# Two attention layers on one core: output's deep weights made in one batch in attention, pairs of exponentials summed by transfers, output's first difference in place, one pool of twelve buffers

## The chip, the cores and the metric

The kernel runs on one core of a Trainium2 chip. The metric is the time of one execution on the device in microseconds; a version's time is the median of its runs. Engines are named as in the profile: PE (TensorE, matmuls), DVE or VectorE, ACT or ScalarE, POOL or GpSimd (here it only issues transfers that add to their destination), SP (SyncE, issues all other transfers).

## The reference

Eight images of 512 channels and 32 x 32 positions, float32, go through two layers. Both do the same: group normalisation over 8 groups, query, key and value projections of 512 x 512, attention with 8 heads of 64 channels over 1024 positions, an output projection with bias, and a residual.

```python
xn = xn * norm_gamma[None, :, None, None] + norm_beta[None, :, None, None]
qkv = jnp.einsum('oc,bchw->bohw', qkv_w, xn) + qkv_b[None, :, None, None]
q, k, v = (qkv[:, 0], qkv[:, 1], qkv[:, 2])
attn = jax.nn.softmax(jnp.einsum('bhds,bhdt->bhst', q, k) * scale, axis=-1)
out = jnp.einsum('bhst,bhdt->bhds', attn, v).reshape(B, C, H, W)
return x + jnp.einsum('oc,bchw->bohw', proj_w, out) + proj_b[None, :, None, None]
```

## The kernel before

One image in one layer is a job; the 16 jobs run in the order (image 0, layer 0), (1, 0), (0, 1), (1, 1), (2, 0) and so on, numbered 0 to 15. Job n passes through three stages on PE.

*V phase* (`v_phase`). The value projection is a two-by-two Strassen-Winograd product: seven products of half matrices, in two banks of PSUM called z, y, v, u in the profile (L494).

*Deep phases* (`deep_phases`, L574 on). Output of job n-1 (called O), then K and Q of job n, each as a two-level product of that kind: seven chains, in the order OUTER = 1, 2, 6, 5, 7, 3, 4, of seven inner products each (L636, two matmuls of 128x256). A chain's result is a part, a tile p of 128x1024, put together from PSUM by ScalarE copies (L646, L648) and VectorE adds of a shared piece s5 (L653, L655). The parts are then added up: for K and Q by VectorE into quarters of k and q (`add`, L667); for O onto the residual x (`more`, L676), by VectorE (L684) or by a transfer that accumulates, issued on POOL (L682, x<-p in the profile). Each chain's left side is a weight tile w of 7 x 128 columns, 448 KB: the *deep weights*. They are fetched ahead on SP (`fetch`, w<-deep). The first time that a kind and layer are used they do not exist yet: then `prepare` makes each of them from loaded blocks by four VectorE adds of 128x128 in the deep phase itself, and stores it for later jobs (deep<-w). The right sides need sums of quarters: for K and Q `deep_steps` (L423 to L429, 128x768, made in attention), for O the class `OutputSums` (os, L534 to L539) and four half-size differences `combine` (L380 to L391) of the attention output q into a tile to.

*Attention* (`Attention`, L850 on). 64 steps: 8 groups (a pair of heads and a half of the positions) by 8 blocks kc of 128 keys. A step is: scores (L878, PE), the exponential e of 128x1024 (L883, ACT), values into the bank po (L909, PE, two steps later: LEAD = 2), and on VectorE acc += e, the softmax's sum (L893 for the first pair, L895 after). With a group's last step `finish` (L914) reduces acc (L925), copies half of po to px on ACT (L931) and adds px and the other half into q (L932: the "q add" below, after which the bank po is free). Every second group the sums are gathered on SP (r<-r), inverted (L956, L957), spread, and q is multiplied by them (L986).

Side work is placed on the 64 steps as *chores*, by `put(step, fn)` in the main loop (L1284 on): raw loads and first-level factors of weights (`first_factors`), the normalisation of the next job, `sums`, `deep_steps`. Work after an attention is ordered by a clock written by hand: `later(at, fn)` sets a due time, `advance(us)` is called after PE's work. So every engine's order is fixed in the program; an instruction that waits holds up what is behind it on its engine. Buffers: `epool` has LEAD + 4 = 6 tiles of 128x1024 for e and p, `ring` has RING = 7 tiles for w.

At the end (`last_proj`) the last job's output is made by a one-level product.

Of the kernel before, what the change touches and what calls it, by code (L numbers as in the profile page):

```python
# [46 lines left out]
RING = 7  # L47
BLOCK = {1: (0, 0), 2: (0, 1), 4: (1, 1)}

# [23 lines left out]
def fast_path(  # L73
# [13 lines left out]
    epool = ctx.enter_context(tc.tile_pool(name="epool", bufs=LEAD + 4))  # L87
# [3 lines left out]
    ring = ctx.enter_context(tc.tile_pool(name="ring", bufs=RING))  # L91
# [70 lines left out]
    def store_factors(w, layer, which):  # L162
        keep = wdram.tile([P, NW, 2, CH], F32, name=f"keep_{which}_{layer}")
        if (which, layer) == (O, 1):
            nc.sync.dma_start(keep, w)
        else:
            for s in (slice(S1, NW), slice(S3, S3 + 1)):
                nc.sync.dma_start(keep[:, s], w[:, s])
        factors[which, layer] = keep
# [3 lines left out]
    def fetch():  # L173


        if not plan or len(held) == RING:
            return
        key = plan.popleft()
        n, which, o = key
        layer = jobs[n][1]  # L180
        w = ring.tile([P, NW, P], F32, tag="w", name=f"w_{which}_{n}_{o}")
        held[key] = w
        if (which, layer, o) in deep:
            nc.sync.dma_start(w, deep[which, layer, o])
        else:
            if o in BLOCK:
                src = raw_block(layer, which, *BLOCK[o])
            else:
                src = factors[which, layer][:, FACTOR[o]]
            nc.sync.dma_start(wide(w), src)  # L190
            if which != V:
                raw.add(key)

    def prepare(key):
        if key not in raw:
            return
        raw.discard(key)
        n, which, o = key
        w = held[key]
        for part in range(4):  # L200
            factor(w, part)
        keep = wdram.tile([P, NW, P], F32, name=f"deep_{which}_{jobs[n][1]}_{o}")
        deep[which, jobs[n][1], o] = keep
        later(1.0, lambda: nc.sync.dma_start(keep, w))

# [194 lines left out]

    def inner_sums(part, direct):
# [141 lines left out]
    class OutputSums:  # L543
# [6 lines left out]
        def steps(self, c):  # L550
            def first():
                n = self.n
                if c == 2:
# [15 lines left out]
                self.pair = sums_of_four(right(self.src, to[0], OUTER[c]), slots)  # L569
# [4 lines left out]
    def deep_phases(n, extra, outs=None, early=()):  # L574
# [5 lines left out]
        chains = [(which, o) for which in ((O, K, Q) if outs else (K, Q)) for o in OUTER]  # L580
        tiles = {}

        def job(which):
            return n - 1 if which == O else n

        def begin(c):
# [3 lines left out]
            if o == OUTER[0] and which != O:  # L590
                name = "k" if which == K else "q"
                dst[which] = acts.tile([P, NC, S], F32, tag=name, name=f"{name}_{n}")
                (kt if which == K else qt)[0] = dst[which]
# [3 lines left out]
            if which == O and c in (3, 4):  # L597
                soon.extend(outs.steps(c + 2))
            e = epool.tile([P, 2, HALF], F32, tag="e", name=f"p_{n}_{c}")
            tiles[which, o] = e  # L600
            s5 = small.tile([P, QT], F32, tag="s5", name=f"s5_{n}_{c}", bufs=3)
            half = (c + len(chains)) % 2
            ends = c + 1 == len(chains)
            names = "yvzu" if ends else ("vyuz", "zyuv")[(c // 2) % 2]
            z, y, u, w = (bank(half, b, f"{b}d_{n}_{c}")[:, :QT] for b in names)
            if which == O:
                r = right(outs.src, to[0], o)
                sums = outs.at[c]
# [26 lines left out]
            def product(i, ps, start):  # L635
                nc.tensor.matmul(  # L636
# [4 lines left out]
            def put(oo, ph, ps):  # L641
                to_ = e[:, oo, ph * QT : (ph + 1) * QT]
# [16 lines left out]
        def end(c):  # L659
# [7 lines left out]
            def add(to_, a, b):  # L667
                outer.append(lambda: nc.vector.tensor_add(to_, a, b))  # L668

            if which == O:  # L670
# [3 lines left out]
                def more(oh, sh, part, moved=False):  # L674
# [5 lines left out]
                    def go():  # L680
                        if moved:
                            nc.gpsimd.dma_start(to_, p(part), accum_op=ALU.add)  # L682
                        else:
                            nc.vector.tensor_add(to_, to_, p(part))  # L684
                        parts[oh, sh] -= 1
# [7 lines left out]
                    waiting[oh, sh] += 1  # L693
                    if not moved:
# [11 lines left out]
                elif o == 6:  # L706
                    add(p(6), p(6), p(1))
# [4 lines left out]
                elif o == 7:  # L712
                    add(p(7), p(7), p(6))
# [7 lines left out]
            d = dst[which]  # L721

            def quarter(oh, sh):
                return d[:, 2 * oh : 2 * oh + 2, sh * HALF : (sh + 1) * HALF]

            if o == 2:
                add(quarter(0, 0), p(1), p(2))
            elif o == 6:
                add(p(6), p(6), p(1))
            elif o == 5:  # L730
                add(quarter(0, 1), p(6), p(5))
            elif o == 7:
                add(p(7), p(7), p(6))
                add(quarter(1, 1), p(7), p(5))
            elif o == 3:
                add(quarter(0, 1), quarter(0, 1), p(3))
            elif o == 4:
                add(quarter(1, 0), p(7), p(4))
# [5 lines left out]
        def thunk(c, j):  # L744
            def go():
                if j == 0:
# [3 lines left out]
                if order[j] in (7, 3):  # L750
# [13 lines left out]
                advance(0.43)  # L764

            return go

# [8 lines left out]
        return [thunk(c, j) for c, j in at]  # L776

    def last_weights(n):
        w = acts.tile([P, NW, 2, CH], F32, tag="deep", name="w_last")
        nc.sync.dma_start(w, factors[O, jobs[n][1]])  # L780
# [77 lines left out]
    class Attention:  # L858
        def __init__(self, n):
# [6 lines left out]
            self.es, self.acc, self.po = {}, {}, {}  # L866

# [20 lines left out]
        def add(self, i):  # L888
            g, kc = self.steps[i]
            acc, e = self.acc, self.es[i]  # L890
# [3 lines left out]
            elif kc > 1:  # L894
                nc.vector.tensor_add(acc[g], acc[g], e)  # L895

        def values(self, i):
# [6 lines left out]
            e = es.pop(i)  # L904
            for h in range(2):
# [8 lines left out]
        def finish(self, g):  # L914
# [4 lines left out]

            n, q, m = self.n, self.q, g % 2  # L920
            hp, sh = self.groups[g]
            to_ = q[:, hp, sh * HALF : (sh + 1) * HALF]
# [6 lines left out]
            p = self.po.pop(g)  # L929
            px = apool.tile([P, HALF], F32, tag="px", name=f"px_{n}_{g}")  # L930
            nc.scalar.copy(px, p[:, 0, :])  # L931
            nc.vector.tensor_add(to_, p[:, 1, :], px)  # L932
# [52 lines left out]
            def normalise():  # L985
                nc.vector.tensor_mul(place, place, box[0])  # L986

            times = (0.0, 0.2, 2.0, 4.0) if ends else (0.0, 7.6, 7.7, 16.2)
# [3 lines left out]
        def run(self, chores):  # L992
# [6 lines left out]
            if 2 in chores:  # L999
                chores[2]()  # L1000
            for i in range(3, len(steps) + LEAD):
# [3 lines left out]
                g, kc = steps[i - LEAD]  # L1005
                if kc == NT - 1:
                    self.finish(g)
                    advance(0.85)
                if i in chores:
                    chores[i]()  # L1010
                advance(1.71)

# [20 lines left out]

    def out_sums(n, outs):
# [3 lines left out]
        def start():  # L1038
            to[0] = acts.tile([P, 4, 2, HALF], F32, tag="k", name=f"to_{n}")
            combine(outs.src, to[0], 0)  # L1040

        def part(i):
            return lambda: combine(outs.src, to[0], i)

        c0, c1, c2, c3, c4 = (outs.steps(c) for c in range(5))
        steps = c0 + [start] + c3 + c1 + [part(1)] + c2 + [part(2)] + c4 + [part(3)]
        times = (0.1, 1.0, 2.5, 4.5, 5.5, 6.5, 7.5, 8.6, 14.0, 15.8, 16.5, 17.5, 19.2, 21.0)
# [20 lines left out]
    def extend_plan(n):  # L1068
        plan.extend((n, V, o) for o in ORDER)
        plan.extend((n - 1, O, o) for o in ORDER)  # L1070
# [32 lines left out]

    def first_factors(put, which_layers):

        box = []

        def start():
            box.append(acts.tile([P, 2, NW, 2, CH], F32, tag="deep", name=f"raw_{len(factors)}"))
            for i, (which, layer) in enumerate(which_layers):  # L1110
                load_blocks(box[0][:, i], layer, which)

        put(2, start)
        at = 9
        for i, (which, layer) in enumerate(which_layers):
            for part in range(4):
                at += 3
                put(at, lambda i=i, part=part: factor(box[0][:, i], part))
            put(at + 1, lambda i=i, which=which, layer=layer: store_factors(
                box[0][:, i], layer, which  # L1120
            ))
# [162 lines left out]
    for n in range(-1, len(jobs)):  # L1284
        last = n + 1 == len(jobs)
        outs = None
        if n >= 0:
            chores = {}

            def put(i, fn):  # L1290
                while i in chores:
                    i += 1
                chores[i] = fn

            if last:
                w = last_weights(n)
                for i, fn in enumerate(last_sums(0)):
                    put(44 + 3 * i, fn)
            else:
                if n == 0:  # L1300
                    first_factors(put, [(O, 0), (V, 1)])
                elif n == 1:
                    first_factors(put, [(K, 1), (Q, 1)])
                elif n == 2:
                    first_factors(put, [(O, 1)])
# [7 lines left out]
                for i, fn in zip(at, steps + sums(n + 1)):  # L1313
                    put(i, fn)
                deep_first = deep_steps(n + 1)
                for at, fn in zip((52, 54, 57, 59), deep_first[4:]):
                    put(at, fn)
                put(61, lambda: (extend_plan(n + 1), [fetch() for _ in range(RING)]))
            assert max(chores, default=0) < NT * len(att.groups)
            att.run(chores)  # L1320
# [22 lines left out]
            if n + 2 < len(jobs):  # L1343
                reads, steps = norm_steps(n + 2)
                extra.extend((15, fn) for fn in reads)
        both = deep_phases(n + 1, extra, outs, deep_first[:4] if outs else ())
# [261 lines left out]
```

## Time and profile before

| | us |
|---|---|
| median of 3 runs (lowest, highest) | 3206.02 (3205.87, 3207.14) |
| span of the profiled execution | 3202.4 |
| PE busy | 3183.5 |
| VectorE busy | 2773.9 |
| ScalarE busy | 1914.3 |
| POOL busy | 99.5 |

The profiled execution's span runs from its first to its last instruction; a run's time holds a few microseconds around that. The granted clock is 0.999 throughout. In the lines of the profile an instruction stands as engine, line, operation, output<-inputs and shape; in a timeline the first two columns are its start and its length, and brackets hold the engine's idle time before it and what ended it. An x4 joins four instructions in a row. In lists of groups the two numbers behind the bar are busy microseconds and mean nanoseconds of one.

### The profile page before, as it was taken

Reading aid. Unit: us, or ns where it says so; the run is one execution under the profiler, and the core shown is the slowest. Engines: PE = TensorE matmul, PEld = TensorE weight load, DVE = VectorE, ACT = ScalarE, POOL = GpSimd, SP = SyncE. Lnnn points to the kernel's source line nnn. Section 1 sums busy time; section 2 is a strip of 40 time slices with the busy share of each in tenths; the row PEclk is TensorE's granted clock in tenths of the full one; section 3 lists DMA queues with packets and bytes.
Section 4 is the critical chain, followed back from the end, with each engine's and each line's share of the span. In section 5 each row is a group of like instructions: output and inputs, shape, how many; then the busy total and the mean of one; then the engine's idle time right before and its main releaser. Section 6 shows DMA issues by size and latency. Waiting matters only on the chain.

```text
span 3202.4 us, 57786 instructions
## 1 busy us (share of the span) xinstructions
PE 3183.5 (99%) x22917; PEld 1862.2 (58%) x22917; DVE 2773.9 (87%) x3990; ACT 1914.3 (60%) x3063; POOL 99.5 (3%) x94
## 2 busy tenths in 40 slices
PE   9999999999999999999999999999999999999999
PEld 7366384663836648366483754837547375573744
DVE  8897999979889798897988889888898888978878
ACT  4746646466565665656656565565656656566564
POOL 0000000000000000000000000000000000000000
PEclk9999999999999999999999999999999999999999
DMA  8234172350713315034170421504316051150611
GB/s 291 74 105 123 49 216 67 95 166 22 213 25 90 89 28 158 22 105 130 31 211 16 117 69 37 149 16 137 101 44 194 16 138 48 49 136 16 174 37 42
DMA packets 156726, 307.80 MB, mean 96 GB/s; under 512 B 34088, under 2 KB 60576, under 8 KB 156192
## 3 DMA queue, kind: packets, MB, share of 16 engines
q1 hardware_dynamic: 139856, 272.05, 26.6%
q0 software_dynamic: 16592, 31.99, 6.1%
q8 instruction: 181, 2.97, 0.4%
q14 instruction: 97, 0.79, 0.1%
HBM read 225.13 MB, written 45.68 MB: 85 GB/s over the span
## 4 chain that ended last, share of the span: by engine, by line
PE 94%; DVE 5%; DMA 1%; issue 0%; ACT 0%; POOL 0%; DVEq 0%; SPq 0%; ACTq 0%; POOLq 0%
PE sc L878 27%; PE po L909 27%; PE zd L636 10%; PE vd L636 10%; PE z L494 6%; PE yd L636 5%; PE ud L636 4%; PE v L494 2%; PE y L494 2%; PE u L494 1%; DVE acc L895 1%; PE z_last L822 0%; DMA x<-p 0%; DMA w<-deep 0%; DVE w L156 0%
## 5 line engine op out<-in xcount | busy, mean ns | idle before, releaser
L883 ACT ACTIVATE e<-sc 128x1024 f32<-128x1024 f32 x1024 | 1045.0, 1024 | 563.6 <-PE sc L878 456.2
L878 PE MATMUL sc<-q,k 64*64 64x512 f32 x8192 | 1058.2, 589 | 0.0
L909 PE MATMUL po<-e,v 64*64 64x512 f32 x8192 | 1057.3, 589 | 0.0
L895 DVE TENSOR_TENSOR acc<-acc,e 128x1024 f32<-128x1024 f32 x768 | 936.2, 1219 | 58.7 <-ACT e L883 12.1
L909 PEld LDWEIGHTS po<-e,v 64*64 64x64 f32 x8192 | 313.2, 133 | 565.7 <-issue 552.9
L878 PEld LDWEIGHTS sc<-q,k 64*64 64x64 f32 x8192 | 311.6, 133 | 562.3 <-issue 544.2
L893 DVE TENSOR_TENSOR acc<-e,e 128x1024 f32<-128x1024 f32 x128 | 156.4, 1222 | 112.2 <-ACT e L883 112.1
L636 PE MATMUL zd<-deep,w 128*128 128x256 f32 x860 | 240.9, 379 | 1.1 <-DVE p L653 0.6
L636 PE MATMUL vd<-deep,w 128*128 128x256 f32 x804 | 224.4, 380 | 4.4 <-ACT yd L438 2.3
L636 PEld LDWEIGHTS zd<-deep,w 128*128 128x128 f32 x860 | 163.1, 190 | 24.7 <-DVE p L653 1.5
L636 PEld LDWEIGHTS vd<-deep,w 128*128 128x128 f32 x804 | 152.3, 190 | 27.2 <-ACT yd L438 2.7
L925 DVE TRANSPOSE_TENSOR_REDUCE r<-acc 128x32 f32<-128x1024 f32 x128 | 158.5, 1238 | 0.6
L682 POOL DMA_DIRECT2D x<-p x61 | 73.4, 1203 | 1974.0 <-ACT p L646 1408.5
L636 PE MATMUL vd<-os,w 128*128 128x256 f32 x420 | 118.2, 380 | 1.6 <-DVE p L655 1.5
L668 DVE TENSOR_TENSOR p<-p,p 128x1024 f32<-128x1024 f32 x94 | 114.2, 1215 | 0.0
L494 PE MATMUL z<-w,t 128*128 128x256 f32 x480 | 110.9, 379 | 0.0
L494 PE MATMUL z<-w,xn 128*128 128x256 f32 x480 | 110.1, 382 | 0.0
L518 ACT COPY v<-z 128x512 f32<-128x512 f32 x32 | 18.8, 586 | 148.7 <-PE z L494 148.7
L494 PEld LDWEIGHTS z<-w,xn 128*128 128x128 f32 x480 | 90.0, 190 | 23.8 <-issue 12.2
L442 ACT COPY ud<-zd 128x256 f32<-128x256 f32 x156 | 55.7, 357 | 76.5 <-PE zd L636 75.5
L653 DVE TENSOR_TENSOR p<-vd,s 128x256 f32<-128x256 f32 x63 | 26.7, 424 | 85.6 <-PE vd L636 85.6
L657 ACT COPY s<-vd 128x256 f32<-128x256 f32 x156 | 58.2, 373 | 70.1 <-PE vd L636 70.1
(242 smaller groups left out, 4193.8 us busy)
## 6 DMA issues: line engine op xcount, KB each, us to landing
w<-deep SPq DMA_DIRECT2D x287, 448.0 KB, 3.6
x<-p POOLq DMA_DIRECT2D x61, 512.0 KB, 6.5
rb<-rd SPq DMA_DIRECT2D x96, 256.0 KB, 4.1
w<-keep SPq DMA_DIRECT2D x84, 256.0 KB, 2.7
deep<-w SPq DMA_DIRECT2D x42, 448.0 KB, 3.3
w<-wqkv_dram SPq DMA_DIRECT2D x57, 256.0 KB, 2.8
x<-x_dram SPq DMA_DIRECT2D x28, 512.0 KB, 6.2
out_dram<-x SPq DMA_DIRECT2D x28, 512.0 KB, 6.0
```

Of the source, the lines that this page charges most:

```text
L442: nc.scalar.copy(u, z)
L494: nc.tensor.matmul(ps[:, ti * CH : (ti + 1) * CH], right(src, tx[0], o)[:, cc, t0 : t0 + P], w[:, cc, :], start=(start and ti == 0 and cc ...
L636: nc.tensor.matmul(ps, lhs[:, FACTOR[i], :], moving[i], start=start, stop=True, skip_group_check=True,)
L657: return chain(product, lambda ps: nc.scalar.copy(s5, ps), put, z, y, u, w)
L668: outer.append(lambda: nc.vector.tensor_add(to_, a, b))
L682: nc.gpsimd.dma_start(to_, p(part), accum_op=ALU.add)
L878: nc.tensor.matmul(sc[h * HD : (h + 1) * HD, j, :], k[r, hp, k0 : k0 + HD], q[r, hp, sh * HALF : (sh + 1) * HALF], start=True, stop=True,)
L883: nc.scalar.activation(e, sc, AF.Exp, scale=SCALE)
L893: nc.vector.tensor_add(acc[g], self.es[i - 1], e)
L895: nc.vector.tensor_add(acc[g], acc[g], e)
L909: nc.tensor.matmul(po[g][j * HD : (j + 1) * HD, h, :], v[r, kc, d0 : d0 + HD], e[r, j, :], start=(kc == 0), stop=(kc == NT - 1),)
L925: nc.vector.tensor_reduce(self.r[:, 0, m, :], self.acc.pop(g).rearrange("p j (b e) -> p (j b) e", e=RP), AX.X, ALU.add, apply_transpose=True,)
```

## The change

Five things are edited.

1. One pool of 12 tiles (PARTS + RING = 6 + 6) for e, p and w. `p_tile` lets at most six parts be held; if there are six, it first issues queued adds.
2. In groups 0 to 6 of each job the exponentials of kc 0 and 1, and of 2 and 3, are added in pairs by accumulating transfers on POOL (`add_pair`, 512 KB each); VectorE's acc holds kc 4 to 7 and takes each pair's sum five steps after the issue (LANDING). The last group is as before. `finish` is split: the q add (`take`) goes ahead of the reduce, and the reduce of paired groups follows their second pair.
3. Output's deep weights of layer 0 and 1 are made in `deep_round`, in the attention of jobs 0 and 2: four raw loads, four operations of 128x512, four of 128x896, seven stores. The first factors of V in layer 1 move to step 43 of job 0, those of K and Q to step 5 of job 1. `last_weights` loads four blocks and two pieces.
4. The first of output's four differences is written over its operand in q, at step 48 of attention (`out_combine`); three are left behind attention, with new times.
5. Parts 2, 6, 5, 7 of K and Q are written straight into the quarters of k and q and added to there. The four `deep_steps` at 52, 54, 57, 59 move to 57 to 60, the last job's `last_sums` from 44 on to 49 on, and the fetch ahead takes six tiles.

The diff also holds code for a deep V (all that stands under `with_v`, `n >= DEEP_V`), which DEEP_V = 99 never reaches with 16 jobs. Against the kernel before, PE has the same instructions in the same order; VectorE has 272 tensor_tensor operations fewer, POOL 224 transfers more, and SP four more.

```diff
-RING = 7
+RING = 6
+PARTS = 6
+LANDING = 5
...
+DEEP_V = 99
+ROUNDS = {0: (O, 0), 2: (O, 1)}
+FIRST = {0: ((V, 1),), 1: ((K, 1), (Q, 1))}
...
-    epool = ctx.enter_context(tc.tile_pool(name="epool", bufs=LEAD + 4))
+    epool = ctx.enter_context(tc.tile_pool(name="epool", bufs=PARTS + RING))
...
-    ring = ctx.enter_context(tc.tile_pool(name="ring", bufs=RING))
...
-        w = ring.tile([P, NW, P], F32, tag="w", name=f"w_{which}_{n}_{o}")
+        w = epool.tile([P, NW, P], F32, tag="e", name=f"w_{which}_{n}_{o}")
...
+    def deep_round(which, layer):
+        box = []
+        def start():
+            t = acts.tile([P, NW, NW, P], F32, tag="deep", name=f"round_{which}_{layer}")
+            box.append(t)
+            for i in range(2):
+                for j in range(2):
+                    nc.sync.dma_start(
+                        t[:, 2 * j + i, 0:4, :].rearrange("p (cc h) o -> p cc (h o)", cc=2),
+                        raw_block(layer, which, i, j),
+                    )
+        def outer_(part):
+            factor(box[0][:, :, 0:4, :], part)
+        def store_outer():
+            w = box[0][:, :, 0:4, :].rearrange("p f (c h) o -> p f c (h o)", c=2)
+            store_factors(w, layer, which)
+        def inner(part):
+            factor(box[0].rearrange("p f a o -> p a f o"), part)
+        def store(o):
+            keep = wdram.tile([P, NW, P], F32, name=f"deep_{which}_{layer}_{o}")
+            nc.sync.dma_start(keep, box[0][:, FACTOR[o]])
+            deep[which, layer, o] = keep
+        first = [lambda part=part: outer_(part) for part in range(4)]
+        second = [lambda part=part: inner(part) for part in range(4)]
+        return start, first, store_outer, second, [lambda o=o: store(o) for o in OUTER]
...
+    def out_right(src, t, o):
+        b11, b12 = src[:, 0:2, :HALF], src[:, 0:2, HALF:]
+        b21, b22 = src[:, 2:4, :HALF], src[:, 2:4, HALF:]
+        return {1: b11, 5: b12, 2: b21, 3: b22}[o] if o in (1, 5, 2, 3) else t[:, {7: 0, 6: 1, 4: 2}[o]]
+    whole = [-1]
+    def out_combine(src, t, part):
+        b11, b12 = src[:, 0:2, :HALF], src[:, 0:2, HALF:]
+        b21, b22 = src[:, 2:4, :HALF], src[:, 2:4, HALF:]
+        if part == 0:
+            nc.vector.tensor_sub(b12, b12, b11)
+        elif part == 1:
+            nc.vector.tensor_sub(t[:, 1], b22, b12)
+        elif part == 2:
+            nc.vector.tensor_sub(t[:, 0], t[:, 1], b11)
+        else:
+            nc.vector.tensor_sub(t[:, 2], b21, t[:, 1])
...
+        def p_tile(key, name, uses):
+            while len(holds) >= PARTS:
+                assert values or outer
+                next_work(len(chains), True)
+            holds[key] = uses
+            return epool.tile([P, 2, HALF], F32, tag="e", name=name)
...
+            if which == O or o not in PLACE:
...
+                uses = {1: 2, 6: 2, 5: 2, 7: 2}.get(o, 1) if which == O else 2 if o == 1 else 1
+                e = p_tile((which, o), f"p_{n}_{c}", uses)
...
+            else:
+                e = quarter(which, *PLACE[o])
...
-            d = dst[which]
-            def quarter(oh, sh):
-                return d[:, 2 * oh : 2 * oh + 2, sh * HALF : (sh + 1) * HALF]
-            if o == 2:
-                add(quarter(0, 0), p(1), p(2))
-            elif o == 6:
-                add(p(6), p(6), p(1))
-            elif o == 5:
-                add(quarter(0, 1), p(6), p(5))
-            elif o == 7:
-                add(p(7), p(7), p(6))
-                add(quarter(1, 1), p(7), p(5))
-            elif o == 3:
-                add(quarter(0, 1), quarter(0, 1), p(3))
-            elif o == 4:
-                add(quarter(1, 0), p(7), p(4))
+            for to_, a in {
+                2: ((2, 1),), 6: ((6, 1),), 7: ((7, 6), (6, 5), (5, 7)), 3: ((6, 3),), 4: ((7, 4),),
+            }.get(o, ()):
+                add(p(to_), p(to_), p(a), a)
...
-        nc.sync.dma_start(w, factors[O, jobs[n][1]])
+        layer = jobs[n][1]
+        load_blocks(w, layer, O)
+        for s in (slice(S1, NW), slice(S3, S3 + 1)):
+            nc.sync.dma_start(w[:, s], factors[O, layer][:, s])
...
+            first = 2 * self.pairs(g)
+            if kc < first:
+                return
+            kc -= first
...
+        def pairs(self, g):
+            return 0 if g + 1 == len(self.groups) else 2
+        def add_pair(self, i):
+            g, kc = self.steps[i]
+            nc.gpsimd.dma_start(self.summed[i], self.summed.pop(i - 1), accum_op=ALU.add)
+            def add():
+                nc.vector.tensor_add(self.acc[g], self.acc[g], self.summed.pop(i))
+                if kc == 2 * self.pairs(g) - 1:
+                    self.reduce(g)
+            self.due[i + LEAD + LANDING] = add
...
+            self.take(g)
+            if not self.pairs(g):
+                self.reduce(g)
...
+                if kc % 2 == 1 and kc < 2 * self.pairs(g):
+                    self.add_pair(i - LEAD)
+                if i in self.due:
+                    self.due.pop(i)()
...
-        steps = c0 + [start] + c3 + c1 + [part(1)] + c2 + [part(2)] + c4 + [part(3)]
-        times = (0.1, 1.0, 2.5, 4.5, 5.5, 6.5, 7.5, 8.6, 14.0, 15.8, 16.5, 17.5, 19.2, 21.0)
+        steps = c0 + c3 + c1 + [parts[0]] + c2 + [parts[1]] + c4 + [parts[2]]
+        times = (0.1, 1.0, 4.5, 5.5, 6.5, 7.5, 8.6, 14.0, 15.8, 16.5, 17.5, 19.2, 21.0)
...
+            def put_round(which, layer):
+                load, first, store_outer, second, stores = deep_round(which, layer)
+                moves[9] = load
+                at = 12
+                for fn in first:
+                    at = put(at + 1, fn)
+                if (which, layer) == (O, 1):
+                    moves[at + 1] = store_outer
+                    at += 4
+                for fn in second:
+                    at = put(at + 1, fn)
+                at = max(at, 30 if n == 0 else 25)
+                for i, fn in enumerate(stores):
+                    at += 1 + i % 2
+                    moves[at] = fn
...
+            def put_first(weights):
+                at = 43 if n == 0 else 5
...
-                    put(44 + 3 * i, fn)
+                    put(49 + 3 * i, fn)
...
+                put(48, lambda q=att.q: out_combine(q, None, 0))
...
-                for at, fn in zip((52, 54, 57, 59), deep_first[4:]):
-                    put(at, fn)
-                put(61, lambda: (extend_plan(n + 1), [fetch() for _ in range(RING)]))
...
+                    for at, fn in zip((57, 58, 59, 60), deep_first[4:]):
+                        put(at, fn)
+                def begin_plan():
+                    extend_plan(n + 1)
+                    for _ in range(RING):
+                        fetch()
```

## The prediction

> **What bounds the kernel now.** I read the page first: busy shares, the chain that ended last, the costly groups, the DMA lines.
>
> ```profile
> span 3202.4 us, 57786 instructions
> ...
> PE 3183.5 (99%) x22917; PEld 1862.2 (58%) x22917; DVE 2773.9 (87%) x3990; ACT 1914.3 (60%) x3063; POOL 99.5 (3%) x94
> ...
> PE 94%; DVE 5%; DMA 1%; issue 0%; ACT 0%; POOL 0%; DVEq 0%; SPq 0%; ACTq 0%; POOLq 0%
> ...
> L895 DVE TENSOR_TENSOR acc<-acc,e 128x1024 f32<-128x1024 f32 x768 | 936.2, 1219 | 58.7 <-ACT e L883 12.1
> ...
> L682 POOL DMA_DIRECT2D x<-p x61 | 73.4, 1203 | 1974.0 <-ACT p L646 1408.5
> ...
> x<-p POOLq DMA_DIRECT2D x61, 512.0 KB, 6.5
> ```
>
> PE is busy 99% and holds 94% of the chain; VectorE's 87% counts only where PE waits for it. The change removes no matmul, so it can win only time in which PE now stands idle, and it loses wherever a new wait reaches PE.
>
> Then the chain of waits in order of time, the first V product of three jobs:
>
> ```profile
> 798.05 3.65 PE z L494 x16
> ...
> 995.91 3.65 PE z L494 x16
> ...
> 1193.76 3.65 PE z L494 x16
> ```
>
> They lie 197.86 and 197.85 us apart, and so to the last job: from job 4 on PE has no stall to win back. The same starts before that (395.24, 597.88) give 202.64 and 200.17, so jobs 2 and 3 lose 4.8 and 2.3 us. PE's timeline over these early jobs shows its waits in brackets, with what ended them:
>
> ```profile
> 197.47 1.99 PE L494 MATMUL v<-w,t 128*128 128x256 f32 x8 [1.18 <-DVE q L932]
> ...
> 224.87 0.70 PE L636 MATMUL vd<-os,w 128*128 128x256 f32 x2 [0.64 <-DVE p L655]
> 228.79 0.70 PE L636 MATMUL zd<-to,w 128*128 128x256 f32 x2 [0.64 <-DVE p L653]
> 246.09 0.70 PE L636 MATMUL vd<-deep,w 128*128 128x256 f32 x2 [2.25 <-ACT yd L438]
> ...
> 628.57 0.59 PE L636 MATMUL zd<-to,w 128*128 128x256 f32 x2
> 629.78 0.70 PE L636 MATMUL vd<-os,w 128*128 128x256 f32 x2 [0.62 <-DVE p L655]
> 630.32 0.59 PE L636 MATMUL yd<-to,w 128*128 128x256 f32 x2
> ...
> 633.71 0.70 PE L636 MATMUL zd<-to,w 128*128 128x256 f32 x2 [0.64 <-DVE p L653]
> ```
>
> Products start 0.43 apart when nothing waits, so behind 628.57 the next was due at 629.00; it came at 629.78, 0.78 late, and the one behind it lost 0.11 more. A wait booked at 0.62 to 0.64 thus costs 0.9.
>
> Last, VectorE at an ordinary attention's end (job 4):
>
> ```profile
> 992.82 5.21 DVE L895 TENSOR_TENSOR acc<-acc,e 128x1024 f32<-128x1024 f32 x4
> 998.06 1.25 DVE L925 TRANSPOSE_TENSOR_REDUCE r<-acc 128x32 f32<-128x1024 f32 x1
> 999.23 0.65 DVE L932 TENSOR_TENSOR q<-po,px 128x512 f32<-128x512 f32 x1
> ```
>
> No idle is marked: VectorE runs full here. The q add ends at 999.88; the V product that writes the bank it reads follows at 999.40 + 1.73 = 1001.13 (eight products of 128x256 after the row at 999.40). The slack is 1.2 us.
>
> **The change, part by part.**
>
> *Output's deep weights out of the deep phases.* Their 28 small adds (284 ns each) a layer sit between PE's products in the first output phases; they delay the adds to p that PE waits for. Without them go, from 0 to 1, the waits at 224.87 and 228.79 (0.9 each) and three unmarked delays that sum to 0.6: -2.4. The 2.25 at 246.09 stays: it waits behind a p buffer that a 9.50 us x<-p transfer held. From 2 to 3 go 629.78 and 633.71: -1.9 with a small one of 0.09. Bounds: 0 (if other work takes the place) to -4.4. I take -4.3, as the adds are the only work there that later jobs, which have no such waits, lack.
>
> *The same work in attention.* In job 0 it adds four VectorE operations of 128x896 (about 1.0 each, between the 0.95 of 128x768 and 1.22 of 128x1024), four raw loads, and seven stores of 448 KB. Those stores go on SP at ten steps of attention, 17.2 us at 1.72 a step, while a store of 448 KB takes 3.3 us to land: 23 us if one after another. SP's queue may fall up to 6 us behind, and behind it queue the three r gathers (1.7 us) of the sums. VectorE's inverse waits for the gathers, and everything behind it on VectorE: the adds of e, which free the buffers for ScalarE's exponentials, and the q add that already costs PE 1.45 at 197.47. The layer-1 factors of V also move from the attention's first half to step 43 and later: four operations of 128x512, 0.65 each, now in its last third. Against this stand 14 adds less (16 us), mostly earlier. Bounds: from -1.45 to +6; I take +3, as the relief comes before the late work. In job 2 the same batch meets no V factors: nothing, while VectorE idles elsewhere in that attention; without that cover as in job 0.
>
> *Pair sums.* Per job 14 adds of 128x1024 leave VectorE (14 x 1.14 = 16 us, 255 us in all) and 14 accumulates of 512 KB are issued on POOL, 224 in all. POOL is 3% busy; 224 x 1.2 = 269 us is 8% more. Software DMA took 6.1% of 16 engines for 31.99 MB; 117 MB more makes 22% more beside the 27% of the other queue. A sum is read five steps (8.6 us) after issue, and x<-p lands in 5.4 to 10.6 us, median 6.5, in the crowded deep phases; attention is emptier, so I take 5.5 and no wait. If they took 9.5, VectorE would stand 0.9 twice in a group, which its 16 us of relief covers except in a job's last group.
>
> That last group is where the loss lies. It keeps its seven adds. Into its eight steps now fall the second pair sum of the group before (1.14; the first falls just ahead) and two more of the four deep differences, moved from 52, 54 to 57, 58 (2 x 0.87); only the own reduce (1.17) goes behind the q add. That is 1.14 + 1.74 - 1.17 = +1.7, less about 0.5, because four chained adds at 1.30 (5.21) are interleaved at 1.14: +1.2, the whole slack of 1.2. PE's wait per job is then 0 (adds overlap better) to 1.7 (the first pair sum slips in as well: 1.2 + 1.14 - 0.6). I take 0.2 over 14 jobs: +2.8, nearest to the zero that the sum gives.
>
> At the end of job 15 the same backlog meets the output's projection, with its four sums moved five steps later (two of 0.65 into the last group): 0 to 1.14 + 1.3 = 2.4; I take +1.8, since VectorE is full from 3163.42 to 3186.
>
> *One pool of twelve, parts in place.* Before, seven w tiles could be ahead and six p tiles had buffers of their own; now six and six share. Two effects. First, w tiles are fetched one later: where x loads lie on SP (jobs 3, 4, 7, 8, 11, 12) that costs 0 to 1.0. Second, in jobs whose output is layer 0 (5, 6, 9, 10, 13, 14) the sixth part of O can come to lie where the second part was, and ScalarE's copy into it must wait until that x<-p has landed. In job 5 the first x<-p is issued at 1025.33, the second at 1032.07 and lands at 1039.3; ScalarE writes the sixth part from 1036.7, and PE, half a chain of seven 0.43 us products from needing that bank, feels what exceeds some 1.6: 0 to 1.0. In other jobs the second lands 11.9 to 12.4 after the first issue, which would hide it. I take 0.2 for twelve jobs: +2.4. K's and Q's in-place adds read parts later in another order; PE's three existing waits of this sort in job 0 are 0.24 to 0.84 (0.4 to 1.0 with restart): 0 to 1.5 for jobs 0 and 1; I take one wait each, 0.9 and 0.6.
>
> *Output's first difference in place*: one 128x1024 subtraction (1.22) leaves the stretch behind attention and enters at step 48, before the full stretch, where the removed adds cover it. Nothing; uncovered, 1.2 in that attention. It was in PE's way in no steady job.
>
> **A rule against it.** Row first: the 61 issues of x<-p took 1200 to 1344 ns each on POOL, beside a VectorE that is 87% busy. The Trainium skill (DMA: Bandwidth & Descriptors, section SWDGE vs HWDGE vs iDMA) says that GpSimd writes such descriptors into SBUF itself and that VectorE locks it out of there in its two-port modes. By that rule an issue could stand for an add, 1.2 us, and the estimate of landing would be 6.7 rather than 5.5; still below 8.6. The rows do not show the lock, and the sum goes without it.
>
> **Sum.** -4.3 + 3.0 + 2.8 + 1.8 + 2.4 + 1.5 = +7.2. On the span: 3202.4 + 7.2 = 3209.6; the median of the runs is 3.6 above the profiled span, so 3213 us.
>
> **Rivals.** What a measurement of this kernel can tell from no change is about 0.2%, 6.4 us.
> (a) *Hidden, no change* (0.36): the steady terms (2.8 + 2.4) and half the others stay under cover. For it: no steady stall before, 16 us of VectorE freed per job. Against it: the slack at attention's end is used up. 3206 - 4.3 + 3 = 3205, anywhere from 3200 to 3212.
> (b) *Faster* (0.08): the freed VectorE also dissolves the waits it is named for elsewhere: 1.45 at 197.47 and 4.8 in job 2. 3206 - 4.3 - 1.45 - 4.8 = 3195.5. Against it: job 2's waits come from layer-1 K and Q adds, which stay.
> (c) *Transfers become the bound* (0.16): if accumulates crowd each other, the sixth part's wait is 1.0 in 6 jobs and w's 1.0 in 6, and the last group is late by 1.2 in 14: 12 + 17 = 29 less 4.3: 3231. It decides once x<-p lands later than 6.2 us in steady jobs (two in a row and 0.6 between them then exceed the 11.4 + 1.6 above). For it: 6.5 median now. Against: the pair sums fall in attention, the others do not.
> (d) *My forecast, slightly slower* (0.40): 3213, own range 3208 to 3222.
>
> **Numbers.** (b) gives faster 0.08. Case (a) and the part of (d) below 3212.4, some 0.07, lie within 0.2%: 0.43; (c) and the rest of (d) are slower: 0.49. The range takes (a) from 3201 and (d), and reaches to (c): 3201 to 3230.
>
> **What would show it.** Right: no wait at products of os in jobs 1 and 3; PE's wait for the q add in job 0 at 3 to 5 us; z starts 197.9 to 198.3 apart; POOL near 330 instructions. Wrong: periods of 197.86 in all steady jobs (then (a)), or over 199 with ACT p or DMA w named (then (c)); VectorE idle at pair sums, ended by DMA acc, would mean that landing outlasts five steps.

## The result, and the profile after

The changed kernel takes 3215.1 us, median of 6 runs (3211.17 to 3219.77), beside 3206.07 (3205.86 to 3207.14) for the kernel before: a ratio of 1.0029 with an interval of 1.0017 to 1.0040. It is slower by 9 us. Its runs also spread over 8.6 us, those of the kernel before over 1.3.

The page of the changed kernel's profile (shares of the span; the queue of POOL's transfers with packets, MB and share of the 16 DMA engines; the chain by engine; a costly group; DMA issues with the median time to landing):

```profile
span 3214.0 us, 58182 instructions
...
PE 3188.8 (99%) x22917; PEld 1868.0 (58%) x22917; DVE 2519.1 (78%) x3718; ACT 1912.8 (60%) x3063; POOL 278.9 (9%) x318
...
q0 software_dynamic: 48848, 149.44, 25.3%
...
PE 90%; DVE 5%; DMA 3%; issue 1%; SPq 0%; ACT 0%; POOL 0%; DVEq 0%; ACTq 0%; POOLq 0%
...
L1128 DVE TENSOR_TENSOR acc<-acc,e 128x1024 f32<-128x1024 f32 x224 | 272.9, 1218 | 7.7 <-DMA e<-e 4.6
...
e<-e POOLq DMA_DIRECT2D x224, 512.0 KB, 4.7
x<-p POOLq DMA_DIRECT2D x61, 512.0 KB, 6.3
```

VectorE is 255 us less busy, as the diff says, and the pair sums are punctual: 224 transfers land in 4.7 us at the median, and VectorE waited for them 4.6 us in all. Yet DMA, which was 1% of the chain, is 3%. Where it comes in is seen on PE. These are lines of PE's timeline in the changed kernel, each a wait that the kernel before did not have or had otherwise:

```profile
193.14 2.85 PE L1148 MATMUL po<-e,v 64*64 64x512 f32 x16 [2.22 <-ACT e L1102]
203.68 2.00 PE L553 MATMUL v<-w,t 128*128 128x256 f32 x8 [1.51 <-DVE q L1171]
...
248.18 0.70 PE L800 MATMUL vd<-deep,w 128*128 128x256 f32 x2 [0.64 <-ACT yd L497]
...
606.53 2.00 PE L553 MATMUL v<-w,t 128*128 128x256 f32 x8 [0.45 <-DVE q L1171]
...
674.97 0.80 PE L800 MATMUL vd<-t,w 128*128 128x256 f32 x2 [1.94 <-DMA w<-deep]
...
1600.54 1.99 PE L553 MATMUL v<-w,t 128*128 128x256 f32 x8 [0.40 <-DVE q L1171]
2590.75 2.00 PE L553 MATMUL v<-w,t 128*128 128x256 f32 x8 [0.46 <-DVE q L1171]
3191.41 2.00 PE L1040 MATMUL z_last<-t_last,w_last 128*128 128x256 f32 x8 [1.48 <-DVE x L1062]
```

The waits on p at 224.87, 228.79, 629.78 and 633.71 are gone. Since PE runs the same matmuls in the same order in both kernels, start can be set against start, matmul by matmul. The changed kernel falls behind by 1.7 us until job 0's attention (0.8 at the program's start, 0.9 in K and Q), by 4.5 more at that attention's end, regains 2.5 and 1.6 in the deep phase from 0 to 1, loses 0.7 from 1 to 2, 0.7 at the end of job 2's attention, regains 1.9 from 2 to 3 and loses 3.6 there again at 674.97, loses 0.7, 0.2, 0.7 and 0.2 in all the jobs after that, and 1.7 in the last projection: 8.8 at PE's last product, against 9.0 between the medians. (The two profiled spans are 11.6 apart; 2.8 of this lies behind PE's last product, where no instruction of the profile shows it.)

In steady jobs little happens. The chain of waits of the changed kernel, first V product of jobs 4, 5 and 6:

```profile
803.35 3.65 PE z L553 x16
...
1001.20 3.65 PE z L553 x16
...
1199.06 3.65 PE z L553 x16
```

197.85 and 197.86 us apart: the same period as before. The loss is in the first four jobs and at the end, but for four waits that lose 1.8 in all.

The chain through job 0's attention shows how transfers got into it (start, length, what; scores and values are left out):

```profile
132.58 1.21 SPq L237
133.83 11.62 DMA deep<-round
146.16 0.84 SPq L156
147.04 0.57 SPq L156
148.17 0.57 SPq L1206
148.78 1.74 SPq L1206
150.56 5.44 DMA r<-r
156.12 0.61 DVE lt L1210
```

The last of the batch's stores (L237) takes 11.62 us to land. V's raw loads (L156) go into the same tile, so SP stands until it has landed; the gather r<-r (L1206) stands behind them on SP, and then takes another 5.44 us, crowded by 1 MB of those loads. VectorE's inverse (lt) waits for it, idle 6.3 us, and every add behind it is late until the attention ends.

### The profile page after: what moved, and what is told of

It is laid out like the page before. It is cut to its first block, busy times and chain, and to the rows that moved or that the text cites. A ratio compares the mean times of both kernels' runs of the same rounds, so it can differ in the third digit from the quotient of the medians.

```text
span 3214.0 us, 58182 instructions
## 1 busy us (share of the span) xinstructions
PE 3188.8 (99%) x22917; PEld 1868.0 (58%) x22917; DVE 2519.1 (78%) x3718; ACT 1912.8 (60%) x3063; POOL 278.9 (9%) x318
## 4 chain that ended last, share of the span: by engine, by line
PE 90%; DVE 5%; DMA 3%; issue 1%; SPq 0%; ACT 0%; POOL 0%; DVEq 0%; ACTq 0%; POOLq 0%
PE sc L1097 25%; PE po L1148 25%; PE vd L800 10%; PE zd L800 10%; PE z L553 7%; PE yd L800 5%; PE ud L800 4%; PE y L553 2%; PE u L553 2%; PE v L553 2%; DVE acc L1118 1%; DMA x<-p 1%; DMA r<-r 1%; DVE acc L1128 1%; DMA deep<-round 0%
## 5 line engine op out<-in xcount | busy, mean ns | idle before, releaser
L1118 DVE TENSOR_TENSOR acc<-acc,e 128x1024 f32<-128x1024 f32 x320 | 390.6, 1221 | 67.0 <-ACT e L1102 60.0
L1125 POOL DMA_DIRECT2D e<-e x224 | 192.6, 860 | 1771.6 <-ACT e L1102 1364.4
L1128 DVE TENSOR_TENSOR acc<-acc,e 128x1024 f32<-128x1024 f32 x224 | 272.9, 1218 | 7.7 <-DMA e<-e 4.6
L1171 DVE TENSOR_TENSOR q<-po,px 128x512 f32<-128x512 f32 x128 | 87.9, 687 | 73.2 <-ACT px L1169 71.7
```

The source lines that it names most:

```text
L1125: nc.gpsimd.dma_start(self.summed[i], self.summed.pop(i - 1), accum_op=ALU.add)
L1128: nc.vector.tensor_add(self.acc[g], self.acc[g], self.summed.pop(i))
```

## The experiments

All are edits of the changed kernel. On the three chips that ran them the kernel before has medians of 3204.5 to 3204.9, some 1.4 us less than in the first comparison, so a time that was expected for 3206 is met when it comes out about 1.4 lower.

**The batch undone.** Output's deep weights are made as before the change: first factors in jobs 0 and 2, small adds in the deep phases. V's factors of layer 1 go back with it, from step 43 of job 0 to behind those of output.

```diff
-ROUNDS = {0: (O, 0), 2: (O, 1)}
-FIRST = {0: ((V, 1),), 1: ((K, 1), (Q, 1))}
+ROUNDS = {}
+FIRST = {0: ((O, 0), (V, 1)), 1: ((K, 1), (Q, 1)), 2: ((O, 1),)}
...
-                at = 43 if n == 0 else 5
+                at = 5
```

> The changed kernel with output's deep weights made as before the change (first factors in the attention of jobs 0 and 2, 28 small adds in the deep phase), all else as changed. Theory 1, the batch's seven stores and V's raw loads behind them crowd job 0's attention: without them VectorE no longer waits 6.25 us for r<-r, PE's waits at 193.14 (2.22) and 203.68 (1.51) fall to 1.5 together, about 4 us won by then with the slow clock behind the first; given back are 2.5 in the deep phase from 0 to 1 and 1.9 from 2 to 3 (waits on VectorE's p): 3214 to 3217 us in all. Theory 2, the pair sums themselves are late: the waits of job 0 stay and the returned adds come on top, 3219 us.

3210.78 us, ratio 1.0022 (1.0012 to 1.0031). Both waits at the end of job 0's attention are gone altogether, and even the 1.35 us that the kernel before lost there; the waits on p are back (0.64 booked, at 225.48, 229.41, 631.05 and 634.98). That is theory 1. The pair sums are all still there, so they alone do not make job 0 late. The time, 3212 with the chip's 1.4 added, is below the expected 3214: the win at job 0's end (5.9 us by start against start) was larger than the 4 allowed for, and near 675 PE waits 1.40 for w<-deep rather than 1.94, with the clock at 1.00 behind it, 2.3 us won that the expectation leaves out.

**No pair sums.**

```diff
-            return 0 if g + 1 == len(self.groups) else 2
+            return 0
```

> The changed kernel with no pair sums by transfers: VectorE adds all eight exponentials again, seven adds in every group. Theory 1 (the batch is at fault in job 0): job 0's end stays at least as late, as VectorE has 16 us more to do there, V products of job 1 start at 196 us or later; steady jobs lose their waits for the q add (0.7 in jobs 8 and 13) since only two differences more and one reduce less fall into the last group; 3212 to 3218 us. Theory 2 (the pair sums are at fault): job 0's wait for e goes, 3208 us.

3211.02 us, 1.0021 (1.0011 to 1.0031). PE's wait for e in job 0 shrinks from 2.22 to 0.74, as theory 2 had it, and the V phase behind it starts at 194.9, a little earlier than in the changed kernel (195.9) and not at 196 or later. But in that V phase PE waits 5.64 us for the q add at 206.00 rather than 1.51, and with the slow clock behind it the run is 4.5 behind the changed kernel there. After one of 0.62 at 408.13 no wait for the q add is left, and z_last waits no more. So the pair sums cost some 3.3 us at the q adds of later jobs and at the end, and save more than that in job 0. In time the two kernels can't be told apart (1.0021 and 1.0029, with intervals that overlap): another 2.9 us comes back near 675, where the wait for w<-deep is 0.84 and the clock stays at 1.00. Theory 2, in which the time falls to 3208, does not hold.

**V's factors into job 1, ahead of K's and Q's.** `put_first` gets its step as an argument.

```diff
-FIRST = {0: ((V, 1),), 1: ((K, 1), (Q, 1))}
+FIRST = {1: ((5, ((V, 1),)), (24, ((K, 1), (Q, 1))))}
```

> The changed kernel with V's layer-1 factors (four raw loads of 256 KB, four operations of 128x512, two stores) moved from step 43 of job 0 into job 1's attention, ahead of K's and Q's, which go to step 24. Theory 1a, V's loads ahead of the gather on SP and V's late VectorE work make job 0's loss: the gather lands in 2 us, VectorE's wait of 6.25 goes, PE's wait at 193.14 too, 3210 to 3212 us. Theory 1b, the seven stores alone do it (they made e<-e take 10.8 us and VectorE wait 3.1): a wait of about 1 us or more on e stays, 3213 to 3215 us.

3214.73 us, 1.0032 (1.0019 to 1.0044): nothing won, but not because job 0 stayed. Its waits are gone, and PE is 4.3 us ahead of the kernel before by 246 us. The loss has moved on; in PE's timeline of this run it stands at the end of job 1's attention, where K's and Q's late work now is:

```profile
395.99 3.69 PE L1148 MATMUL po<-e,v 64*64 64x512 f32 x16 [5.77 <-ACT e L1102]
```

Theory 1a holds for job 0: the batch's stores alone cost PE nothing there, though VectorE still waits 0.7 and 3.0 us for two pair sums, and 1.9 for r<-r instead of 6.3. The edit takes V's four late operations (2.7 us on VectorE) away together with its loads; no run parts the two. The expected time was wrong, since I had not asked what the moved work would do in job 1.

**The deep differences earlier.**

```diff
-                    for at, fn in zip((57, 58, 59, 60), deep_first[4:]):
+                    for at, fn in zip((50, 52, 54, 56), deep_first[4:]):
...
-                    put(49 + 3 * i, fn)
+                    put(44 + 3 * i, fn)
```

> The changed kernel with the four deep differences at steps 50, 52, 54, 56 rather than 57 to 60, and the last sums from 44 on as before the change. Theory 1, the moved differences fill VectorE in the last group: the q add ends about 2 us earlier in steady jobs, the 0.7 us waits of V in jobs 3, 8 and 13 go and most of the 1.7 at z_last; 3212 us. Theory 2, the second pair sum and the reduce behind it do it: the waits stay, 3215 us.

3210.28 us, 1.0019 (1.0010 to 1.0029). The waits of V in jobs 3, 8 and 13 are gone, and z_last waits 0.47 rather than 1.48: theory 1. In job 0 the edit costs: the differences need the tile that V's raw blocks hold there, and PE's wait for e grows from 2.22 to 5.09 us at 197.71 (2 us of it lost by job 1's V phase, as the wait for the q add goes).

**All adds of output's part 5 on VectorE.** In jobs 1 and 3 one of these adds went by POOL, in both kernels; those were the jobs whose deep phases were full of small adds.

```diff
-                    more(1, 1, 5, m in (0, 2))
+                    more(1, 1, 5)
```

> The changed kernel with one transfer less in the deep phases of jobs 1 and 3: the add of part 5 of output onto x, which POOL makes there alone in these two jobs, goes back to VectorE as in all other jobs. Theory P: the two x<-p that land only after 11 us in job 3 crowd with this extra one, and they gate SP's w fetches; without it the wait of PE for w<-deep near 675 (1.94, with half clock behind it some 3.5 in all) falls below 0.5, as in jobs 7 and 11: 3 us won, 3212. Theory Q: the pool's six w tiles make it (one fetched later): the wait stays above 1, 3215.

3211.26 us, 1.0021 (1.0012 to 1.0030). The 1.94 us wait for w<-deep in job 3 is gone, and so is the one that was left at 248.18 in job 1. POOL's timeline, first the changed kernel and then this run:

```profile
637.48 1.21 POOL L886 DMA_DIRECT2D x<-p  x1 [5.42 <-ACT yd L497]
639.99 1.20 POOL L886 DMA_DIRECT2D x<-p  x1 [1.30 <-ACT p L818]
646.09 1.19 POOL L886 DMA_DIRECT2D x<-p  x1 [4.91 <-ACT p L818]
649.13 1.19 POOL L886 DMA_DIRECT2D x<-p  x1 [1.85 <-ACT p L816]
```

```profile
637.52 1.19 POOL L886 DMA_DIRECT2D x<-p  x1 [4.88 <-DVE os L598]
647.23 1.20 POOL L886 DMA_DIRECT2D x<-p  x1 [8.51 <-ACT yd L497]
650.84 1.20 POOL L886 DMA_DIRECT2D x<-p  x1 [2.41 <-DVE p L823]
```

With the transfer at 639.99 the last two land after 11.0 and 11.5 us, without it after 7.5 and 6.6. SP's stores of x wait for them, and w<-deep queues behind those stores and the loads of the next x. The chain of the changed kernel:

```profile
649.13 11.51 DMA x<-p
...
660.66 3.80 DMA out_dram<-x
...
666.28 8.64 DMA w<-deep
...
674.97 0.80 PE vd L800 x2
```

So theory P holds: without the transfer there is no wait. It does not clear the pool of twelve, which is unchanged here. The kernel before has that transfer too, its last two x<-p land after 10.6 us each, and its chain shows the same late fetch:

```profile
666.12 8.21 DMA w<-deep
674.38 1.13 PE vd L636 x4
```

It books a wait of only 0.17, because it needs this tile one chain of seven products (3.0 us) later: the product at 674.97 in the changed kernel is the one at 671.03 in the kernel before. One w tile fewer is held ahead, so the same fetch comes one chain too late. By these rows the wait takes both, the transfer and the sixth tile in place of the seventh; a run with seven was not made. With the small adds back in the deep phase (the batch undone) the wait is still 1.40.

**V's factors into job 1, behind K's and Q's.**

```diff
-FIRST = {0: ((V, 1),), 1: ((K, 1), (Q, 1))}
+FIRST = {1: ((5, ((K, 1), (Q, 1))), (26, ((V, 1),)))}
```

> The changed kernel with V's layer-1 factors moved into job 1's attention behind K's and Q's (loads at step 26, K's and Q's at 5 as changed). If late loads and late VectorE work in job 1 made the 5.8 us wait near 396 of the run with V first, that wait goes here and job 0 stays clean: 4 to 5 us won, 3210 to 3211. If any V work in job 1 is too much, a wait for e of over 2 us shows at the end of job 1's attention, 3214.

3206.17 us, 1.0007 (0.9998 to 1.0016). No wait at the end of either attention: job 0 clean, job 1 clean. By the ratios, 1.0029 and 1.0007, some 7 us were won where 4 to 5 were expected. The profiled execution is the fastest of ten that reach up to 3213.38; its wait for w<-deep in job 3 is 1.17.

**The last three edits together** (V behind K and Q, differences early, part 5 on VectorE).

> All three together: V behind K and Q in job 1, the deep differences at 50 to 56 and the last sums from 44, no extra transfer in jobs 1 and 3. If the waits are what the runs so far show, the first product of job 2's V phase starts 4 us or more before that of the kernel before the change, no steady job waits, z_last waits 0.6, and the time is 3199 to 3203 on a chip where the kernel before takes 3204 to 3206: faster than both. If the waits only move on (as they did from job 0 to job 1), 3207 or more.

3200.72 us, 11 runs within 3199.09 to 3201.84; ratio 0.9987 (0.9978 to 0.9996) to the kernel before. It is faster than both by 4 us and some 13. No wait of PE for the q add, for e or for w is left; the chain of waits of this run gives

```profile
791.83 3.65 PE z L553 x16
...
989.69 3.65 PE z L553 x16
```

so job 4 starts 6.2 us before that of the kernel before (798.05) and 11.5 before that of the changed one. The spread of the runs is 2.8 us.

**The same without pair sums.**

> The run with the three edits once more, but without pair sums by transfers: VectorE adds all exponentials. If the pair sums bought time that PE sees (theory F: freed VectorE matters in the early jobs' attentions, where batch and norm work lie), job 0's end waits for the q add by 1.4 us (as in the kernel before) up to 4 more, 3202 to 3205 us. If VectorE's 255 us lay off PE's path everywhere (theory N), the time is that of the run with pair sums or less: 3199 to 3201, and z_last waits no longer.

3209.45 us, 1.0014 (1.0005 to 1.0023), 8.7 slower than with them: theory F, but by more than the 3202 to 3205 expected for it, and at another place. Job 0 loses only 1 us at the q add (0.80 booked). Nearly all the rest is in job 1, which now holds twelve factor operations of K, Q and V:

```profile
395.89 3.69 PE L1148 MATMUL po<-e,v 64*64 64x512 f32 x16 [4.85 <-ACT e L1102]
```

Behind job 3 only two waits of 0.69 and 0.40 (at 2033.67 for ScalarE, at 2260.68 for w<-deep) are new, and the wait at z_last is gone. What the pair sums free is worth next to nothing in a steady job; it pays in an attention that other work is packed into.

## Why the prediction was right, and where it was not

The forecast was 3213 us, slightly slower, and 3215 came. By its own steps:

*Deep weights out of the deep phases*: -2.4 and -1.9 predicted, -2.5 and -1.9 measured. The waits named are those that went, and undoing the batch brought them back.

*The same work in job 0's attention*: +3.0 predicted (bounds -1.45 to +6), +4.5 measured. The path was as told: stores on SP, r gathers behind them, VectorE's inverse idle (6.3 us; up to 6 was allowed), adds and q add late. Two things were sized wrongly. The stores did not come at ten steps; they left SP within 7 us, as soon as the factors were made, and landed up to 11.62 us later. And V's factors, which I priced as 2.6 us of late VectorE work alone, also brought the raw loads that held SP: with V's factors elsewhere the same stores cost nothing at PE. Between the two runs VectorE's wait for r<-r differs by 4.3 us and V's late work by 2.7, so the loads look like the larger part; that is an estimate, as both moved together. The slow clock told of below falls into this stretch but is no part of the 4.5: VectorE's timeline marks no idle from 164.70 to the q add at 202.94, for which PE waits in any case. The run with all adds on VectorE has the same wait for e (2.21) without the slow clock, then waits 3.16 for the q add rather than 1.51, and starts the next product at 203.50, against 203.68.

*The last group*: the q add was to end 1.2 us later than before; in job 4's attention it ends at 1006.14, 5.01 us behind the first V product of job 5 (1001.13 in PE's timeline), where it was 4.04 (999.88 behind 995.84), so 1.0 later. VectorE's timeline of the changed kernel there:

```profile
1001.65 3.88 DVE L1118 TENSOR_TENSOR acc<-acc,e 128x1024 f32<-128x1024 f32 x3
1005.45 0.69 DVE L1171 TENSOR_TENSOR q<-po,px 128x512 f32<-128x512 f32 x1
1006.05 1.24 DVE L1183 TRANSPOSE_TENSOR_REDUCE r<-acc 128x32 f32<-128x1024 f32 x1
```

The reduce stands behind the q add, and the slack of 1.2 holds, narrowly. In the V phases of jobs 3, 8 and 13 it did not: some 0.7 each, 2.1 in all for the 2.8 predicted, but as three waits and not as 0.2 in fourteen jobs. Ahead of job 8's, VectorE had waited 0.75 for an r<-r that took 5.5 us beside a pair sum. That the moved differences fill the group is shown by the run with them earlier, that the pair sums do by the run without them; either alone fits.

*The end*: +1.8 predicted, 1.7 measured.

*One pool of twelve*: +2.4 predicted, as 0.2 in twelve jobs. In the steady jobs 0.4 came, in two waits (0.2 each). But the 3.6 at 674.97 belongs here in part: the prediction has a w tile fetched one later, at 0 to 1.0 where x loads lie on SP, with job 3 among the jobs. This is a term mis-sized: the wait that it names came once, as 1.94 with 1.6 of slow clock behind it, beyond its bound. *Parts in place*: 1.5 predicted; 0.9 in job 0, and 0.7 net from 1 to 2 behind two new waits.

*Pair sums in time*: 5.5 us assumed, 4.7 measured, and VectorE waited for three of 224, two of them beside the batch's stores (8.4 and 10.8 us to land). The lock that the prediction weighed does not show beside this kernel's VectorE work, most of it additions of two inputs: an issue of e<-e took 0.86 us on POOL, less than the 1.20 of x<-p.

What was missing in the sum: -1.6 at 246.09, which I said would stay (ScalarE's wait for a p buffer fell from 3.20 to 1.59, and PE's behind it from 2.25 to 0.64; which edit did it no run parts), and most of the +3.6 at 674.97. There I had not seen the transfer, which is in both kernels, nor the slow clock. So the total is nearer than its parts, and that is luck. Measured less predicted: +1.5 at job 0's end, +3.6 in job 3 and +0.8 at the start on one side; -1.6 at 246.09, -2.0 for the pool and -0.7 for the last group on the other: 1.6 together, from the sum's 7.2 to the 8.8 measured.

Of the signs that the prediction named, the waits at products of os in jobs 1 and 3 went, and POOL has 318 instructions for "near 330". PE's wait for the q add in job 0 is 1.51 rather than 3 to 5, with 2.22 for e ahead of it. The periods are 197.85 and 197.86 in most steady jobs and longer where jobs 8 and 13 wait. The former was its sign for rival (a): a loss of 0.2 in each of these jobs, taken twice in the sum, did not come.

Rival (a), all hidden, held for the steady jobs and failed in the early ones. Rival (c), transfers as the bound, was wrong about the place: not in each job's deep phase but once in job 0 and once in job 3. Of rival (b), faster, the run with three edits shows how much there was: 4 us.

## What to carry to other kernels

Work that is moved off the critical path takes its transfers along: ask which queue they stand in, which tile they wait for, and which small transfer then stands behind them. Here a batch of stores, with loads that waited for its tile and an 8 KB gather behind them, cost PE as much (4.5 us) as taking the moved arithmetic away had won (4.4). A buffer fewer shows only where a fetch is late already, so look for the wait at the most crowded place (job 3 here) and not at an average one. A detour that a load forced can be taken out when the load goes (the transfer of part 5, some 3 us). And time freed on an engine that does not set the pace is worth only what is then packed into it.

## What the runs showed of the hardware

A long wait of PE can cost more than itself. Windows of the changed kernel around the wait at 193.14 (stretch, length, busy time of PE, PEld, DVE, ACT, POOL, the granted clock, DMA share, GB/s):

```profile
189.00:191.00 2.00, 1.92 (x20) 0.46 (x12) 2.00 (x3) 0.00 (x0) 0.00 (x0) 1.00 0.86 203
194.00:196.00 2.00, 2.00 (x13) 0.34 (x9) 2.00 (x3) 0.00 (x0) 0.00 (x0) 0.54 0.42 151
196.00:198.00 2.00, 2.00 (x6) 1.68 (x7) 2.00 (x3) 0.58 (x1) 0.00 (x0) 0.61 0.16 25
198.00:200.00 2.00, 2.00 (x11) 1.77 (x10) 2.00 (x3) 0.57 (x1) 0.00 (x0) 1.00 0.31 107
```

The clock falls to about half for some 3.5 us behind a wait of 2.22, and PE's products fall 1.7 us further behind; behind the wait of 1.94 at 674.97 it is 1.6. (At 193.14 the q add hides this, as told above; at 674.97 it is paid.) Length alone does not decide it. The run with all adds on VectorE has two waits in the same stretch:

```profile
192.96 2.00 PE L1148 MATMUL po<-e,v 64*64 64x512 f32 x16 [2.21 <-ACT e L1102]
...
203.50 2.41 PE L553 MATMUL v<-w,t 128*128 128x256 f32 x8 [3.16 <-DVE q L1171]
```

Behind the first the clock stays at 1.00, behind the second it is 0.50 from 205 to 207. And in the kernel before, 2.25 us at 246.09 left the clock at 1.00, and a wait of 2.81 at the same place in job 3 of the run with V first was followed by full pace. The Trainium skill (TensorE: Matmul & The Clock Gate, Part 1: The HAM clock gate) sets this clock by the activity in a window of about 3.4 us that runs freely, so that the moment of a change depends on where in the window the first matmul lands. If the same goes for a gap, it fits the rows here, in which equal waits end differently; but the page lets the clock fall after an idle window, and here waits of 1.94 and 2.22 us were enough. Waits that come out now with this and now without it may be part of why the changed kernel's runs spread over 8.6 us and those of the run without long waits over 2.8; that was not tried by itself, and the kernel before spreads over 6.0 us in the 27 runs beside the latter.
